# A four-layer graph network in one kernel: scores of two layers moved into the values' buffer, masks taken from the codes

## The chip, the cores and the metric

The kernel runs on one core of a Trainium2 chip, as one program with one launch. The metric is the device time in microseconds (us); lower is better. Four of the core's engines do the arithmetic: TensorE (PE) multiplies matrices and turns tiles, VectorE (DVE) and ScalarE (ACT) work element by element, GpSimd (POOL) does small things here. Each engine takes its instructions in a fixed order and waits for the others by semaphores. SyncE (SP) issues nearly all DMA transfers, also in a fixed order.

## The reference

32 graphs of 512 nodes with 256 features go through four layers. Each layer normalises x, takes the positive part, runs a graph attention over the same adjacency matrix, and adds the result to x. What matters for this change is the attention of layers 1 and 2, whose logits are a sum of one number per row and one per column, and the masks:

```python
    # layer 1
    src = Wh @ a1
    dst = Wh @ a2
    e = src[:, :, None] + dst[:, None, :]
    e = jnp.where(e > 0, e, ALPHA * e)
    e = jnp.where(adj > 0, e, NEG_INF)
    attention = jax.nn.softmax(e, axis=-1)
    h_prime = jnp.einsum('bij,bjf->bif', attention, Wh)

    # layer 2
    logits = s[:, :, None] + d[:, None, :]
    e = jnp.where(adj != 0, jnp.exp(-jax.nn.leaky_relu(logits, negative_slope=ALPHA)), jnp.zeros((), dtype=Hh.dtype))
    rowsum = jnp.sum(e, axis=-1, keepdims=True)
    h_prime = jnp.einsum('bnm,bmo->bno', e, Hh) / rowsum
```

Layers 0 and 3 have full products for their logits; they use the same adjacency. The adjacency holds only 0 and 1.

## The kernel before, in words

**Work and tiles.** A graph has 4 tiles of 128 nodes (NT = 4). All arithmetic is in 32-bit floats; masks and codes are bfloat16. Per graph, PE makes the products of layer 0 (bank_f, bank_v0, bank_q, bank_a0, bank_z, bank_o), the values of layers 1 and 2 (bank_v1, bank_v2) with their attentions (bank_a1, bank_a2), and the products of layer 3 (bank_f3, bank_v3, bank_s3, bank_w3, bank_a3). Results land in eight banks of PSUM, and a bank is free again once ACT or DVE has read it out.

**The order.** The code of a graph doesn't issue instructions; it records operations with an assumed cost, what they come after, and which buffers they use (`op`). A planner (class `Plan`) then lists the operations of all 32 graphs together: each has a due time that is worked back from its graph's end, the most urgent one that is ready goes first, and a buffer must be free when its first user starts. It tries several distances between the graphs' due times and keeps the one that its own replay likes best. Several graphs are thus in flight at once (FLIGHT = 5), and any edit of operations or buffers can change the order of everything else. On the chip each engine keeps the planned order.

**Buffers.** Most tiles of 4 KB a partition share one pool of pages (PAGES = 35): x, e (half of the attention matrix each), masks, hT and so on. The values of a layer lie in one of four buffers v of [128, 4, 259] floats (VALUES = 4): two columns ahead (LEAD = 2), 256 values, and a last column of ones that gives the row sums of the attention matmul. Layers 0 to 2 read it from column 2 on, 257 columns; layer 3 uses all 259.

**Scores of layers 1 and 2.** The weights l1_aug and l2_aug have 258 columns: 256 for the values and two more for the two numbers per node. One matmul group per tile (`scored_values`, L669) gives all 258 columns in a bank. ACT copies 256 of them to v (L676), DVE copies the two last to a score buffer (L673), one of five [128, 132] tiles, one for each graph in flight. From there `leaky_exp_t` makes the row of 512 column numbers on all partitions. For the first two and last two graphs PE turns the scores, tile by tile, into a bank (bank_r, L693). For the others DVE turns blocks of 32x32 (sT, L697), a small DMA collects the row in DRAM (L701), and another spreads it to all partitions (L706). Then ACT makes Prelu of the row plus a bias per partition, which is the other score (L710), and the exponential (L713).

**Codes and masks.** Per graph, DVE turns the adjacency into codes (L511), DMAs transpose them (codeT, L514), and DVE makes mask0 (L522), mask1 (L931) and mask3 (L1001), a page each. Layer 1 keeps or crushes an element of e by a minimum with mask1 (L934); layer 2 multiplies with "code is not zero" straight from codeT (L961).

Of the kernel before, what the change touches and what calls it, by code (L numbers as in the profile page):

```python
# [11 lines left out]
F32 = mybir.dt.float32  # L12
# [3 lines left out]
AF = mybir.ActivationFunctionType  # L16
ALU = mybir.AluOpType
PSUM = bass.MemoryType.PSUM

P = 128  # L20
EPS = 1e-5
ALPHA = 0.2
NEG_INF = -(2.0**53)
TINY = 2.0**-100
HUGE = 2.0**100
LEAST = 2.0**-126
LOWEST = -3.0e38

# [177 lines left out]
def kernel(  # L206
# [31 lines left out]
    nc = tc.nc  # L238
# [2 lines left out]
    HC = H // P  # L241
    HALF = H // 2
    FLIGHT = 5
    PAGES, VALUES = 35, 4
    TURNED = 2
    LEAD = 2

# [88 lines left out]
    def load(dst, src, *keys):  # L336

        loads.append(prepare("G", G_LOAD, [], lambda: nc.gpsimd.dma_start(out=dst() if callable(dst) else dst, in_=src),
                             *keys, size=P * HC * H * 4 if keys else 4096))
        return loads[-1]  # L340

    def rows_of(w):
        return w.rearrange("(c p) k -> p c k", p=P)
# [9 lines left out]
    def transposed(w_sb, dst, after, *keys):  # L353
        done = []
        for c in range(HC):
            key = f"bank{next(banks)}"

            def turn(c, key):
                for r in range(HC):
                    nc.tensor.transpose(W[key][:, r * P : (r + 1) * P], w_sb()[:, r, c * P : (c + 1) * P], ident)  # L360

            def out_of(c, key):
                nc.vector.tensor_copy(dst()[:, c, :], W[key][:, : HC * P])

            a = prepare("PE", pe(nt=HC), after, partial(turn, c, key), key, *keys)
            done.append(prepare("V", V_ADD, [a], partial(out_of, c, key), key, *keys))
        return done

    def product(dst, wT, rhs, cols, after, *keys):

        done = []
        for d in range(HC):
            key = f"bank{next(banks)}"

            def multiply(d, key):
                for c in range(HC):
# [38 lines left out]
    for n, dst, w, key in (("w0", w0_s, w0, "raw9"), ("att", att_s, att_w, "raw10")):  # L415
# [8 lines left out]
    l1_sb, l2_wt, l3_sb, a12_sb, wt3, awt, m3_sb, l3_w1_sb = (raw(f"raw{i}") for i in range(8))  # L424
    l3_wide = raw("raw8", H + 2)
    a = [load(l1_sb, rows_of(l1_w), "raw0")]
    ready["l1"] = transposed(l1_sb, lambda: l1_aug[:, :, :H], a, "raw0")
    a += [load_column(l1_ac, l1_a.rearrange("n o -> (n o)"))]
    ready["l1"] += product(lambda d: l1_aug[:, d, H : H + 2], l1_sb,
                           lambda c: l1_ac.rearrange("p (o c) -> p c o", o=2)[:, c, :], 2, a, "raw0")  # L430
    a = [load(l2_aug[:, :, :H], rows_of(l2_w))]
    a = ready["l2"] = a + transposed(lambda: l2_aug[:, :, :H], l2_wt, a, "raw1")
    a = a + [load_column(l2_ac, l2_a.rearrange("o n -> (o n)"))]
    ready["l2"] = a + product(lambda d: l2_aug[:, d, H : H + 2], l2_wt,
                              lambda c: l2_ac.rearrange("p (o c) -> p c o", o=2)[:, c, :], 2, a, "raw1")

    t = transposed(l3_sb, wt3, [load(l3_sb, rows_of(l3_w), "raw2")], "raw2", "raw4")
# [17 lines left out]
    for i in range(VALUES):  # L455
        v = const.tile([P, NT, LEAD + H + 1], F32, tag=f"v{i}", name=f"v{i}")
        nc.gpsimd.memset(v[:, :, LEAD + H :], 1.0)
        v_bufs.append(v)

    score_bufs = []  # L460
    for i in range(FLIGHT):
        s = const.tile([P, P + NT], F32, tag=f"scores{i}", name=f"scores{i}")
        nc.gpsimd.memset(s, 0.0)
        score_bufs.append(s)


    def graph(b, adj_before, x_before):
# [4 lines left out]
        def op(engine, cost, after, emit, *keys, size=0, weights=()):  # L472
            return plan.op(engine, cost, after, emit, b, T.uses(keys) + W.uses(weights), size)

        def two(g):
            return slice(2 * g, 2 * g + 2)
# [7 lines left out]
        def e(l, c):  # L484

            return T[f"e{l}_{c // 2}"][:, c % 2, :]
# [21 lines left out]
                o["after"] += got_adj[-1:]  # L508

        def classes(g):  # L510
            nc.vector.tensor_scalar(T["code"][:, two(g), :], T["adj"][:, two(g), :], -1.0, 2.0, ALU.max, ALU.min)  # L511

        def turn_code(t):
            nc.sync.dma_start_transpose(out=T["codeT"][:, :, t * P : (t + 1) * P], in_=T["code"][:, t, :])  # L514
# [4 lines left out]
            coded += [op("D", D_TURN, [code], partial(turn_code, t), "code", "codeT") for t in (2 * g, 2 * g + 1)]  # L519

        def mask0():
            nc.vector.tensor_scalar(T["mask0"], T["codeT"], 1.0, TINY, ALU.is_equal, ALU.max)  # L522

        m0 = op("V", V_HALF, coded, mask0, "codeT", "mask0")

# [126 lines left out]
            return (lambda x: [sums[x][0]] if x in sums else list(after),  # L652
                    lambda x: d(sums[x][1]) if x in sums else b(*plain[x]))

        def scores_of():

            return score_bufs[T.places["slot"]["number"]]

        def scored_values(l, hs, w_aug, ready):


            cols = w_aug.shape[2]
            vs, ss = [], []
            for t in range(NT):
                key = f"bank_v{l}{t}"

                def product(t, key):
                    for c in range(HC):
                        nc.tensor.matmul(T[key][:, :cols], T[f"hT{l}"][:, c, t * P : (t + 1) * P],  # L669
                                         w_aug[:, c, :], start=(c == 0), stop=(c == HC - 1))  # L670

                def scores(t, key):
                    nc.vector.tensor_copy(scores_of()[:, 32 * t : P + 1 + t : P - 31 * t], T[key][:, H:cols])  # L673

                def values(t, key):
                    nc.scalar.copy(T[f"v{l}"][:, t, LEAD : LEAD + H], T[key][:, :H])  # L676

                a = op("PE", pe(n258=4), [hs[t]] + ready, partial(product, t, key), key, f"hT{l}")
                ss.append(op("V", V_TINY, [a], partial(scores, t, key), key))
                vs.append(op("A", A_HALF, [a], partial(values, t, key), key, f"v{l}"))  # L680
            return vs, ss

        def leaky_exp_t(l, ss, sign):

            turned = b < TURNED or b >= B - TURNED
            key = f"bank_r{l}" if turned else f"row{l}"
            line = []  # L690

            def turn(t):
                nc.tensor.transpose(T[key][:, t * P : (t + 1) * P],  # L693
                                    scores_of()[:, 32 * t : 32 * t + 1].to_broadcast([P, P]), ident)

            def squares():
                nc.vector.transpose(T[f"sT{l}"], scores_of()[:, :P])  # L697

            def collect():
                line.append(dram.tile([N], F32, tag=f"row_{T.places['slot']['number']}", name=f"row{l}_{b}"))  # L700
                nc.sync.dma_start(out=line[0].rearrange("(t g j) -> g t j", t=NT, j=32),  # L701
                                  in_=T[f"sT{l}"][0:P:32, :].rearrange("g (t j) -> g t j", t=NT))

            def spread():
                d = line[0]
                nc.sync.dma_start(out=T[key][:, 0, :], in_=bass.AP(tensor=d.tensor, offset=d.offset, ap=[[0, P], [1, N]]))  # L706

            def leaky(c):
                row = T[key] if turned else T[key][:, 0, :]
                nc.scalar.activation(e(l, c), row, AF.Prelu, bias=scores_of()[:, P + c : P + c + 1], alpha=ALPHA)  # L710

            def exp(c):
                nc.scalar.activation(e(l, c), e(l, c), AF.Exp, scale=sign)  # L713

            a = None
            if turned:
                for t in range(NT):
                    a = op("PE", pe(nt=1), [ss[t], a], partial(turn, t), key)
            else:
                a = op("V", V_SQUARES, ss, squares, f"sT{l}")  # L720
                a = op("D", D_OUT, [a], collect, f"sT{l}")
                a = op("D", D_SPREAD, [a], spread, key, size=P * N * 4)
            ls = [op("A", A_PRELU if turned else A_PRELU2, [a], partial(leaky, c), key, f"e{l}_{c // 2}") for c in range(NT)]
            return [op("A", A_EXP, [x], partial(exp, c), f"e{l}_{c // 2}") for c, x in enumerate(ls)]

        def attend(l, es, vs, use):
# [200 lines left out]
            xs += [op("V", V_ADD, [a], partial(add_z, 2 * g + j), "z0", "x") for j in range(2)]  # L927


        def mask1():  # L930
            nc.vector.tensor_scalar(T["mask1"], T["codeT"], HUGE, TINY, ALU.mult, ALU.max)  # L931

        def masked1(c):
            nc.vector.tensor_tensor(e(1, c), e(1, c), T["mask1"][:, c, :], ALU.min)  # L934

        hs = normed(1, xs)
        m1 = op("V", V_HALF, [m0, hs[0]], mask1, "codeT", "mask1")
        vs, ss = scored_values(1, hs, l1_aug, ready["l1"])
        es = leaky_exp_t(1, ss, 1.0)
        es = [op("V", V_MASK, [a, m1], partial(masked1, c), "mask1", f"e1_{c // 2}") for c, a in enumerate(es)]  # L940

        def second(t, a, key):
            def sums():
# [10 lines left out]


        hs = normed(2, xs)
        vs, ss = scored_values(2, hs, l2_aug, ready["l2"])
        es = leaky_exp_t(2, ss, -1.0)

        def masked2(c):  # L960
            nc.vector.scalar_tensor_tensor(e(2, c), T["codeT"][:, c, :], 0.0, e(2, c), ALU.not_equal, ALU.mult)  # L961
# [224 lines left out]
```

## Time and profile before

| what | us |
|---|---|
| device time, median of 3 runs | 2376.73 |
| lowest and highest of the 3 | 2376.35, 2377.58 |
| device time of the profiled execution | 2375.45 |
| its span, from first to last instruction | 2373.7 |
| busy POOL | 251.6 |
| longest wait of PE in the page's groups | 6.0 (all of L736's together) |

A profile page gives busy time per engine as a share of the span, the span in slices, the chain of work that ended last, and groups of instructions by line and shape, each with its count, busy time, mean duration in ns and the idle time just before it with what ended it. Timelines list instructions in order of time. A busy PE isn't PE at its peak: matmuls are pipelined, so the distance from the start of one to the start of the next says more than the duration of each (a 257-column matmul of L736 has a mean duration of 381 ns).

### The profile page before, as it was taken

Reading aid. Unit: us, or ns where it says so; the run is one execution under the profiler, and the core shown is the slowest. Engines: PE = TensorE matmul, PEld = TensorE weight load, DVE = VectorE, ACT = ScalarE, POOL = GpSimd, SP = SyncE. Lnnn points to the kernel's source line nnn. Section 1 sums busy time; section 2 is a strip of 40 time slices with the busy share of each in tenths; the row PEclk is TensorE's granted clock in tenths of the full one; section 3 lists DMA queues with packets and bytes.
Section 4 is the critical chain, followed back from the end, with each engine's and each line's share of the span. In section 5 each row is a group of like instructions: output and inputs, shape, how many; then the busy total and the mean of one; then the engine's idle time right before and its main releaser. Section 6 shows DMA issues by size and latency. Waiting matters only on the chain.

```text
span 2373.7 us, 36569 instructions
## 1 busy us (share of the span) xinstructions
PE 2347.7 (99%) x11590; PEld 1985.6 (84%) x11590; DVE 2056.8 (87%) x6330; ACT 1720.1 (72%) x3386; POOL 251.6 (11%) x319
## 2 busy tenths in 40 slices
PE   7999999999999999999999999999999999999998
PEld 5887888888888888888888888888888888888887
DVE  6787899888898888988888988889888889888799
ACT  4566777777777777777777777777777777766785
POOL 3000010111001010101110111001011100100110
PEclk9999999999999999999999999999999999999999
DMA  7421332333333233332323334233233333321221
GB/s 188 94 54 30 87 86 65 85 79 69 85 70 89 69 67 87 78 84 70 85 61 85 74 72 87 65 85 78 66 88 77 71 83 74 89 54 41 49 47 43
DMA packets 432017, 178.72 MB, mean 75 GB/s; under 512 B 386288, under 2 KB 403824, under 8 KB 431824
## 3 DMA queue, kind: packets, MB, share of 16 engines
q1 hardware_dynamic: 426464, 158.03, 29.8%
q0 software_dynamic: 5216, 18.23, 2.3%
q8 instruction: 92, 1.51, 0.3%
q14 instruction: 101, 0.83, 0.1%
q10 hardware_dynamic: 144, 0.13, 0.0%
HBM read 67.64 MB, written 16.89 MB: 36 GB/s over the span
## 4 chain that ended last, share of the span: by engine, by line
PE 94%; DVE 3%; ACT 2%; DMA 0%; issue 0%; SPq 0%; POOL 0%; DVEq 0%; ACTq 0%
PE bank_a L736 35%; PE bank_z L893 9%; PE bank_v L669 9%; PE bank_o L911 5%; PE bank_s3p L1025 5%; PE bank_q0p L848 4%; PE bank_f3p L757 4%; PE bank_v0p L783 4%; PE bank_f0p L757 4%; PE bank_w3p L783 4%; PE bank_q0q L848 3%; PE bank_s3q L1025 3%; PE bank_v3p L783 2%; PE bank_v3q L783 2%; ACT e L710 1%; ACT e L713 0%
## 5 line engine op out<-in xcount | busy, mean ns | idle before, releaser
L736 PE MATMUL bank_a<-v,e 128*128 128x257 f32 (+1 forms) x4096 | 979.8, 381 | 6.0 <-DVE e L823 3.0
L736 PEld LDWEIGHTS bank_a<-v,e 128*128 128x128 f32 x4096 | 758.3, 190 | 155.3 <-issue 55.3
L566 ACT COPY hT<-planesT 128x512 uint16<-128x512 uint16 x508 | 380.8, 766 | 52.0 <-DMA planesT<-planes 51.6
L539 POOL TENSOR_TENSOR rstd<-ve,mhalf 128x2 f32<-128x2 f32 x256 | 215.9, 871 | 1875.1 <-DVE ve L536 1584.4
L546 ACT ACTIVATE xn<-x,off,rstd 128x256 f32<-128x256 f32 x512 | 276.0, 596 | 39.2 <-DVE off L542 39.0
L669 PE MATMUL bank_v<-l_aug,hT 128*128 128x258 f32 x1024 | 252.8, 381 | 2.1 <-ACT e L710 1.1
L893 PE MATMUL bank_z<-e,y 128*128 128x512 f32 x512 | 240.6, 592 | 0.0
L551 DVE COPY planes<-xn 128x512 uint16<-128x512 uint16 x508 | 205.7, 418 | 23.0 <-DMA planesT<-planes 17.2
L669 PEld LDWEIGHTS bank_v<-l_aug,hT 128*128 128x128 f32 x1024 | 191.7, 190 | 30.5 <-ACT e L710 1.5
L532 DVE BATCH_NORM_STATS2 st<-x 128x6 f32<-128x256 f32 x512 | 209.0, 408 | 4.1 <-DMA x<-in_x_dram 4.0
L710 ACT ACTIVATE e<-row,scores 128x512 f32<-128x512 f32 x224 | 150.7, 713 | 16.3 <-DMA row<-row 16.0
L893 PEld LDWEIGHTS bank_z<-e,y 128*128 128x128 f32 x512 | 96.9, 190 | 68.0 <-issue 57.9
L713 ACT ACTIVATE e<-e 128x512 f32<-128x512 f32 x256 | 150.3, 624 | 0.0
L676 ACT COPY v<-bank_v 128x256 f32<-128x256 f32 x256 | 90.2, 376 | 71.5 <-PE bank_v L669 67.7
L911 PE MATMUL bank_o<-w_sb,zT 128*128 128x256 f32 x512 | 116.2, 379 | 0.0
L1032 DVE SCALAR_TENSOR_TENSOR e<-bank_s3p,v,mask 128x256 f32<-128x256 f32 x256 | 111.2, 476 | 2.7 <-PE bank_s3p L1025 1.9
L533 DVE BATCH_NORM_AGGREGATE mv<-st 128x2 f32<-128x6 f32 x512 | 93.1, 182 | 17.5
L911 PEld LDWEIGHTS bank_o<-w_sb,zT 128*128 128x128 f32 x512 | 97.0, 190 | 13.4
L1077 ACT ACTIVATE e<-e 128x512 f32<-128x512 f32 x128 | 78.1, 629 | 22.7 <-DVE e L1074 22.0
L915 DVE SCALAR_TENSOR_TENSOR z<-bank_o,rs,b_sb 128x256 f32<-128x256 f32 x128 | 56.0, 479 | 40.7 <-PE bank_o L911 40.1
L974 ACT ACTIVATE y<-bank_a,rs 128x256 f32<-128x256 f32 x128 | 54.7, 476 | 49.4 <-DVE rs L970 25.9
L1071 ACT ACTIVATE e<-e,zero 128x512 f32<-128x512 f32 x128 | 84.9, 711 | 6.6 <-DVE crest L1049 6.6
(189 smaller groups left out, 4414.9 us busy)
## 6 DMA issues: line engine op xcount, KB each, us to landing
adj<-in_adj_dram SPq DMA_DIRECT2D x128, 256.0 KB
x<-in_x_dram SPq DMA_DIRECT2D x31, 512.0 KB
out_dram<-y POOLq DMA_DIRECT2D x31, 512.0 KB, 3.5
row<-row SPq DMA_DIRECT2D x56, 256.0 KB
planesT<-planes SPq DMA_TRANSPOSE x508
codeT<-code SPq DMA_TRANSPOSE x128
crest<-crest SPq DMA_TRANSPOSE x64
row<-sT SPq DMA_DIRECT2D x56, 2.0 KB
```

The source lines that it names most:

```text
L532: nc.vector.bn_stats(T[f"st{l}"][:, t, :], T["x"][:, t, :])
L539: nc.gpsimd.tensor_tensor(T[f"rstd{l}"][:, two(g)], T[f"ve{l}"][:, two(g)], mhalf[:, two(g)], ALU.pow)
L546: nc.scalar.activation(T[f"xn{l}"][:, t, :], T["x"][:, t, :], AF.Relu, bias=T[f"off{l}"][:, t : t + 1], scale=T[f"rstd{l}"][:, t : t + 1])
L551: nc.vector.tensor_copy(T[f"planes{l}_{t}"], bits)
L566: nc.scalar.copy(bits[:, :, :, t * P : (t + 1) * P], T[f"planesT{l}_{t}"].rearrange("p (b c) n -> p b c n", b=2))
L669: nc.tensor.matmul(T[key][:, :cols], T[f"hT{l}"][:, c, t * P : (t + 1) * P], w_aug[:, c, :], start=(c == 0), stop=(c == HC - 1))
L736: nc.tensor.matmul(T[key][:, : LEAD + H + 1 - lead], e(l, c)[:, t * P : (t + 1) * P], T[f"v{l}"][:, c, lead:], start=(c == 0), stop=(c == ...
L757: nc.tensor.matmul(p[:, : N // 2], w[:, x - 1, :], right(x), start=fresh, stop=True, skip_group_check=True)
L783: nc.tensor.matmul(p[:, j * k : (j + 1) * k], right(x)[:, j * P : (j + 1) * P], w[:, x - 1, :], start=fresh and j == 0, stop=True, skip_gr ...
L893: nc.tensor.matmul(T[f"bank_z{k}"], T["y0"][:, c, k * P : (k + 1) * P], e(0, c), start=(c == 0), stop=(c == NT - 1))
L911: nc.tensor.matmul(T[key][:, j * H : (j + 1) * H], T["zT"][:, k, t * P : (t + 1) * P], w1_sb[:, k, :], start=(k == 0), stop=(k == HC - 1))
L1025: nc.tensor.matmul(p[:, j * N // 2 : (j + 1) * N // 2], left(x)[:, j * P : (j + 1) * P], right(x), start=fresh and j == 0, stop=True, skip ...
```

## The change

Four things are changed together. The two score columns move to the front of the weights, so that they land in the two leading columns of the values' buffer by the same ACT copy that brings the values; the score buffers and DVE's score copies are gone, and what read the scores reads v. The codes are the adjacency times 2^96 instead of a clamped adjacency, so that layer 1 can take its minimum with max(code, 2^-100) in one operation, and mask1 is gone. The pool of pages has one page less, and there are five buffers of values instead of four. The dependences follow: the transposes and Prelus wait for ACT's copies, where they waited for DVE's.

```diff
-HUGE = 2.0**100
+HUGE = 2.0**96
...
-    PAGES, VALUES = 35, 4
+    PAGES, VALUES = 34, 5
...
-    ready["l1"] = transposed(l1_sb, lambda: l1_aug[:, :, :H], a, "raw0")
+    ready["l1"] = transposed(l1_sb, lambda: l1_aug[:, :, 2:], a, "raw0")
...
-    ready["l1"] += product(lambda d: l1_aug[:, d, H : H + 2], l1_sb,
+    ready["l1"] += product(lambda d: l1_aug[:, d, 0:2], l1_sb,
...
-    score_bufs = []
-    for i in range(FLIGHT):
-        s = const.tile([P, P + NT], F32, tag=f"scores{i}", name=f"scores{i}")
-        nc.gpsimd.memset(s, 0.0)
-        score_bufs.append(s)
...
         def classes(g):
-            nc.vector.tensor_scalar(T["code"][:, two(g), :], T["adj"][:, two(g), :], -1.0, 2.0, ALU.max, ALU.min)
+            nc.vector.tensor_scalar(T["code"][:, two(g), :], T["adj"][:, two(g), :], HUGE, None, ALU.mult)
...
         def mask0():
-            nc.vector.tensor_scalar(T["mask0"], T["codeT"], 1.0, TINY, ALU.is_equal, ALU.max)
+            nc.vector.tensor_scalar(T["mask0"], T["codeT"], HUGE, TINY, ALU.is_equal, ALU.max)
...
-                def scores(t, key):
-                    nc.vector.tensor_copy(scores_of()[:, 32 * t : P + 1 + t : P - 31 * t], T[key][:, H:cols])
-
                 def values(t, key):
-                    nc.scalar.copy(T[f"v{l}"][:, t, LEAD : LEAD + H], T[key][:, :H])
+                    nc.scalar.copy(T[f"v{l}"][:, t, :cols], T[key][:, :cols])
 
                 a = op("PE", pe(n258=4), [hs[t]] + ready, partial(product, t, key), key, f"hT{l}")
-                ss.append(op("V", V_TINY, [a], partial(scores, t, key), key))
                 vs.append(op("A", A_HALF, [a], partial(values, t, key), key, f"v{l}"))
-            return vs, ss
+            return vs
...
             def turn(t):
                 nc.tensor.transpose(T[key][:, t * P : (t + 1) * P],
-                                    scores_of()[:, 32 * t : 32 * t + 1].to_broadcast([P, P]), ident)
+                                    T[v][:, t, 0:1].to_broadcast([P, P]), ident)
 
             def squares():
-                nc.vector.transpose(T[f"sT{l}"], scores_of()[:, :P])
+                nc.vector.transpose(T[f"sT{l}"].rearrange("p (t j) -> p t j", t=NT), T[v][:, :, 0:32])
...
             def leaky(c):
                 row = T[key] if turned else T[key][:, 0, :]
-                nc.scalar.activation(e(l, c), row, AF.Prelu, bias=scores_of()[:, P + c : P + c + 1], alpha=ALPHA)
+                nc.scalar.activation(e(l, c), row, AF.Prelu, bias=T[v][:, c, 1:2], alpha=ALPHA)
...
-                    a = op("PE", pe(nt=1), [ss[t], a], partial(turn, t), key)
+                    a = op("PE", pe(nt=1), [vs[t], a], partial(turn, t), key, v)
             else:
-                a = op("V", V_SQUARES, ss, squares, f"sT{l}")
+                a = op("V", V_SQUARES, vs, squares, f"sT{l}", v)
...
-        def mask1():
-            nc.vector.tensor_scalar(T["mask1"], T["codeT"], HUGE, TINY, ALU.mult, ALU.max)
-
         def masked1(c):
-            nc.vector.tensor_tensor(e(1, c), e(1, c), T["mask1"][:, c, :], ALU.min)
+            nc.vector.scalar_tensor_tensor(e(1, c), T["codeT"][:, c, :], TINY, e(1, c), ALU.max, ALU.min)
 
         hs = normed(1, xs)
-        m1 = op("V", V_HALF, [m0, hs[0]], mask1, "codeT", "mask1")
-        vs, ss = scored_values(1, hs, l1_aug, ready["l1"])
-        es = leaky_exp_t(1, ss, 1.0)
-        es = [op("V", V_MASK, [a, m1], partial(masked1, c), "mask1", f"e1_{c // 2}") for c, a in enumerate(es)]
+        vs = scored_values(1, hs, l1_aug, ready["l1"])
+        es = leaky_exp_t(1, vs, 1.0)
+        es = [op("V", V_MASK, [a], partial(masked1, c), "codeT", f"e1_{c // 2}") for c, a in enumerate(es)]
```

The weights of layer 2 are shifted like those of layer 1, and layer 2 calls `scored_values` and `leaky_exp_t` in the same new way.

More of the change, by code (lines that the diff above doesn't have):

```diff
@@ L426 @@
     a = [load(l1_sb, rows_of(l1_w), "raw0")]
-    ready["l1"] = transposed(l1_sb, lambda: l1_aug[:, :, :H], a, "raw0")
+    ready["l1"] = transposed(l1_sb, lambda: l1_aug[:, :, 2:], a, "raw0")
     a += [load_column(l1_ac, l1_a.rearrange("n o -> (n o)"))]
-    ready["l1"] += product(lambda d: l1_aug[:, d, H : H + 2], l1_sb,
+    ready["l1"] += product(lambda d: l1_aug[:, d, 0:2], l1_sb,
                            lambda c: l1_ac.rearrange("p (o c) -> p c o", o=2)[:, c, :], 2, a, "raw0")
-    a = [load(l2_aug[:, :, :H], rows_of(l2_w))]
-    a = ready["l2"] = a + transposed(lambda: l2_aug[:, :, :H], l2_wt, a, "raw1")
+    a = [load(l2_aug[:, :, 2:], rows_of(l2_w))]
+    a = ready["l2"] = a + transposed(lambda: l2_aug[:, :, 2:], l2_wt, a, "raw1")
     a = a + [load_column(l2_ac, l2_a.rearrange("o n -> (o n)"))]
-    ready["l2"] = a + product(lambda d: l2_aug[:, d, H : H + 2], l2_wt,
+    ready["l2"] = a + product(lambda d: l2_aug[:, d, 0:2], l2_wt,
                               lambda c: l2_ac.rearrange("p (o c) -> p c o", o=2)[:, c, :], 2, a, "raw1")
@@ L653, in block_sums @@
                     lambda x: d(sums[x][1]) if x in sums else b(*plain[x]))
-        def scores_of():
-            return score_bufs[T.places["slot"]["number"]]
         def scored_values(l, hs, w_aug, ready):
             cols = w_aug.shape[2]
-            vs, ss = [], []
+            vs = []
             for t in range(NT):
@@ L670, in product, with leaky_exp_t @@
                                          w_aug[:, c, :], start=(c == 0), stop=(c == HC - 1))
-                def scores(t, key):
-                    nc.vector.tensor_copy(scores_of()[:, 32 * t : P + 1 + t : P - 31 * t], T[key][:, H:cols])
                 def values(t, key):
-                    nc.scalar.copy(T[f"v{l}"][:, t, LEAD : LEAD + H], T[key][:, :H])
+                    nc.scalar.copy(T[f"v{l}"][:, t, :cols], T[key][:, :cols])
                 a = op("PE", pe(n258=4), [hs[t]] + ready, partial(product, t, key), key, f"hT{l}")
-                ss.append(op("V", V_TINY, [a], partial(scores, t, key), key))
                 vs.append(op("A", A_HALF, [a], partial(values, t, key), key, f"v{l}"))
-            return vs, ss
-        def leaky_exp_t(l, ss, sign):
+            return vs
+        def leaky_exp_t(l, vs, sign):
             turned = b < TURNED or b >= B - TURNED
             key = f"bank_r{l}" if turned else f"row{l}"
-            line = []
+            line, v = [], f"v{l}"
             def turn(t):
                 nc.tensor.transpose(T[key][:, t * P : (t + 1) * P],
-                                    scores_of()[:, 32 * t : 32 * t + 1].to_broadcast([P, P]), ident)
+                                    T[v][:, t, 0:1].to_broadcast([P, P]), ident)
             def squares():
-                nc.vector.transpose(T[f"sT{l}"], scores_of()[:, :P])
+                nc.vector.transpose(T[f"sT{l}"].rearrange("p (t j) -> p t j", t=NT), T[v][:, :, 0:32])
             def collect():
@@ L717, in leaky_exp_t @@
                 for t in range(NT):
-                    a = op("PE", pe(nt=1), [ss[t], a], partial(turn, t), key)
+                    a = op("PE", pe(nt=1), [vs[t], a], partial(turn, t), key, v)
             else:
-                a = op("V", V_SQUARES, ss, squares, f"sT{l}")
+                a = op("V", V_SQUARES, vs, squares, f"sT{l}", v)
                 a = op("D", D_OUT, [a], collect, f"sT{l}")
                 a = op("D", D_SPREAD, [a], spread, key, size=P * N * 4)
-            ls = [op("A", A_PRELU if turned else A_PRELU2, [a], partial(leaky, c), key, f"e{l}_{c // 2}") for c in range(NT)]
+            ls = [op("A", A_PRELU if turned else A_PRELU2, [a], partial(leaky, c), key, v, f"e{l}_{c // 2}") for c in range(NT)]
             return [op("A", A_EXP, [x], partial(exp, c), f"e{l}_{c // 2}") for c, x in enumerate(ls)]
@@ L956, in graph @@
         hs = normed(2, xs)
-        vs, ss = scored_values(2, hs, l2_aug, ready["l2"])
-        es = leaky_exp_t(2, ss, -1.0)
+        vs = scored_values(2, hs, l2_aug, ready["l2"])
+        es = leaky_exp_t(2, vs, -1.0)
         def masked2(c):
```

## The prediction

> **What bounds the kernel now.** I read the page first, then TensorE's timeline over the whole span, then the stretches in which it has gaps, then the groups by shape. The page's busy shares, and the first pieces of its chain:
>
> ```profile
> span 2373.7 us, 36569 instructions
> PE 2347.7 (99%) x11590; PEld 1985.6 (84%) x11590; DVE 2056.8 (87%) x6330; ACT 1720.1 (72%) x3386; POOL 251.6 (11%) x319
> ...
> PE 94%; DVE 3%; ACT 2%; DMA 0%; issue 0%; SPq 0%; POOL 0%; DVEq 0%; ACTq 0%
> ```
>
> PE carries 94% of the chain. [...] So I priced PE by its pace instead, from the chain in order of time:
>
> ```profile
> 107.11 3.45 PE bank_o L911 x16
> ...
> 334.22 12.22 PE bank_a L736 x56
> ...
> 522.03 2.62 PE bank_v L669 x12
> ...
> 1859.03 12.14 PE bank_a L736 x56
> ```
>
> 12.14 us for 56 is 217 ns for one 257-column matmul, 3.45/16 is 216 ns for 256 columns, and it is the same at 334 us as at 1859 us. The median distance from one start to the next, kind by kind: 217 (257 and 258 columns), 218 (259), 216 (256), 429 (512), 111 (128 and 129). Times the counts: attention 3072 x 217 + 1024 x 218 = 889.8 us; values of layers 1 and 2 1024 x 217 = 222.2; bank_z 512 x 429 = 219.6; bank_o 512 x 216 = 110.6; bank_f 882 x 216 = 190.5; bank_q and bank_s 1764 x 216 = 381.0; the 2660 of 128 or 129 columns x 111 = 295.3; set-up, first graph and bank_r some 33. Sum 2342.1 us. The rest of the span is 2373.7 - 2342.1 = 31.6: 9.1 before the first matmul, 16.7 in gaps or slow matmuls, 5.8 at the end (from the last one's pace to the last instruction). Where the 16.7 lie, by stretches of 75 us: 4.75 in 0 to 75 (net of early matmuls under their kind's median), 3.4 in 150 to 225, 0.5 in 300 to 375, 0.15 around 1760, 0.6 in 2025 to 2100, 7.3 from 2175 on; from 375 to 1725 us every stretch has less than 0.02. The windows agree (columns: stretch, its length, busy us and count of PE, weight load, DVE, ACT, POOL, clock, DMA share, GB/s):
>
> ```profile
> 150.00:225.00 75.00, 72.37 (x365) 60.94 (x364) 58.54 (x181) 47.68 (x95) 5.00 (x7) 1.00 0.15 27
> ...
> 900.00:975.00 75.00, 75.00 (x375) 63.92 (x374) 66.47 (x206) 57.09 (x113) 8.82 (x11) 1.00 0.31 75
> ...
> 2250.00:2325.00 75.00, 72.22 (x391) 63.06 (x390) 68.67 (x220) 58.35 (x126) 7.72 (x9) 1.00 0.21 43
> ```
>
> So in the long middle no other engine costs anything, and a change that leaves PE's instructions alone can only win or lose at the two ends. The largest gap of the ramp, on ACT and then PE:
>
> ```profile
> 192.94 1.35 ACT L710 ACTIVATE e<-row,scores 128x512 f32<-128x512 f32 x2
> 194.16 1.16 ACT L713 ACTIVATE e<-e 128x512 f32<-128x512 f32 x2
> 195.20 1.34 ACT L710 ACTIVATE e<-row,scores 128x512 f32<-128x512 f32 x2
> 196.42 1.15 ACT L713 ACTIVATE e<-e 128x512 f32<-128x512 f32 x2
> 197.46 0.84 ACT L884 ACTIVATE y<-bank_a,rs 128x256 f32<-128x256 f32 x2
> ...
> 197.99 0.70 PE L736 MATMUL bank_a<-v,e 128*128 128x257 f32 x2 [2.16 <-ACT y L884]
> ```
>
> PE waits for graph 3's tanh, which frees a bank; that tanh stands in ACT's order behind 16 Prelus and exponentials of graphs 1 and 2.
>
> **The change, part by part.** The groups concerned:
>
> ```profile
> L961 DVE SCALAR_TENSOR_TENSOR e<-codeT,e 128x512 f32<-128x512 bf16 x128 | 85.8, 680 | 2.5 <-ACT e L713 1.8
> ...
> L934 DVE TENSOR_TENSOR e<-e,mask 128x512 f32<-128x512 f32 x128 | 82.3, 682 | 3.1 <-ACT e L713 3.0
> ...
> L673 DVE COPY scores<-bank_v 128x2 f32<-128x2 f32 x256 | 35.6, 151 | 15.8 <-ACT v L676 7.6 <-PE bank_v L669 6.6
> ...
> L931 DVE TENSOR_SCALAR mask<-codeT 128x2048 bf16<-128x2048 bf16 x32 | 21.7, 677 | 0.0
> ```
>
> - Removed on DVE: 256 score copies, 35.6 us, and 32 mask1, 21.7 us: 57.3 of 2056.8, so DVE falls from 87% to 84%. Beside a full PE in the middle this is worth 0; it is worth something only at the ends.
> - masked1 becomes the form of L961: 680 against 682 ns, 0. [...]
> - The codes lose one of two operations over the same 1024 elements: 683 ns kept as the dear end, 64 x 0.1 us saved as the cheap one, all hidden: 0. The masks of layers 0, 2 and 3 keep their cost.
> - ACT's values copy takes 258 columns for 256. L1012 copies 258 in 375 ns, L676 256 in 376: 0.
> - The two score columns now lead the weights, so PE writes the same 258 columns; transposes onto bank_r stay 32 x 109 ns. The attention still reads 257 columns from column 2. PE's 2342.1 stay.
> - The 32x32 transposes read with a stride of 259 elements instead of a packed tile. No row shows that; nearest is L697's 301 ns. Bounds 0 and +0.3 us each on DVE, taken 0: a second 301 ns on 56 of them is 17 us, less than the 57.3 removed.
> - The new wait: row transposes, bank_r transposes and the Prelu biases need ACT's copy (376 ns, in ACT's order) where they needed a 151 ns copy on DVE. That is 0.2 us more in itself, plus what stands ahead in ACT's order. Behind it on DVE stand masks and sums, behind the row's two DMAs on SP the next transposes of planes and codes. One such route of layer 2 in the old trace: squares at 972.57, its two DMAs at 972.89 and 976.69, the Prelus at 980.30, the first matmul on them at 984. By the instruction order and the paces above, the work PE has between the last bank_v of a layer and its first attention matmul is 20.0 to 23.5 us before and 19.2 to 21.8 after (graphs 10, 11, 20, 21). The route costs 0.4 copy + 0.3 + 3.8 + 3.6 + two Prelus and two exponentials 2.4 + mask 0.7 = 11.2. Some 8 us stay for queueing, so 0.
> - One page less, one v buffer more: in the changed order graph 2's layer 1 uses the fifth buffer while four are held. POOL drops five memsets of 0.2 us and gains one, at 1 to 2 us, when it waits until 7.47 anyway: 0.
>
> What does count is the new order that the planner draws from all this. Up to the first attention matmul the engines' orders are unchanged, so the 9.1 and the 3.1 us wait for the first mask stay. That wait also drops the clock: most of the next ten matmuls run some 210 ns slow. [...] These 4.75 are kept but for 0.6 of the small waits at 60 to 66 us. In the ramp, graph 3's tanh now stands ahead of graph 2's Prelus and behind joins and value copies. To size this I counted, in each order, ACT's work (at the durations of the rows) from the PE result that it needs up to an instruction, against PE's work before the user of that instruction: the worst user in the ramp is 4.4 us short before, and has 0.1 us to spare after. Of 3.4 us I take away 3.0, and leave 0.4 for an addition in graph 3's bank_f that is 0.3 us short. The 0.5 at 308 us is a bank_f that waits for DVE's addition, the 0.6 at 2077 an attention that waits for layer 2's mask on DVE; there the same count for DVE goes from 0.9 short to 0.3 spare. I let both go (bounds: 0 and 1.1 us).
>
> The tail: 7.3 us of gaps with DVE 92% busy. Some 16 score copies and one mask1 leave it, 3 us of DVE at most; but the last copies end at 2274, and the chain after 2285 is Prelus, sums and stores that stay. Against it, both last graphs take the transpose route four times, and at 2272 to 2274 ACT's copy came 1.6 us after DVE's. Steps with under 1.5 us of PE work between producer and user fall from 132 to 120 in the last 150 us. The count above has the worst user of ACT 6.3 us short before and 6.2 after, of DVE 2.0 and 1.9. Bounds: 3 us gained, 4 x 1.6 = 6.4 lost; I take 1 gained.
>
> Sum: 0.6 + 3.0 + 0.5 + 0.6 + 1.0 = 5.7 us. The profiled execution took 2375.45 (1.75 around its span), so it would take 2369.8; from the median of 2376.73, 1.3 above that one, 2371.0.
>
> **Rivals.**
> - B, the stalls only move: another tight place appears wherever one goes, PE is full anyhow. For it: 99% busy; against: the tanh is plainly reordered. 2376.7, within 2.
> - C, the tail shortens too, because DVE is its bound and each removed copy waits for PE: 3 us in the tail instead of 1, and the small start waits wholly gone: 2368. Against: the removed work isn't in the last 90 us.
> - D, slower: the score route is late. Deciding point: values copy to attention over some 19 us instead of 11.2, by ACT's queue (57 of 75 us busy) and SP's. ACT already waited 21 of 56 times for the row, 16.0 us in all, without any cost to PE. If each of 56 routes cost PE 0.3 us, 17 us less the 5.7: 2388.
> - [...]
>
> **Numbers.** My forecast A 0.50 (2368.5 to 2373.5), C 0.20, B 0.18, D 0.12. Measurements of this kernel tell 0.2%, that is 4.75 us, from no change: under 2372.0 is faster, over 2381.5 slower. Two thirds of A (0.33) and C (0.20) are faster: 0.53; a third of A and B: 0.35; D: 0.12. The range reaches over C and B and leaves out D: 2366 to 2379.
>
> **What would show it.** PE's paces unchanged and the middle without gaps; no 2.2 us gap on PE at some 195 us with a tanh behind Prelus; the 3.1 us gap at 28.5 still there; DVE busy some 1999 us; the tail's gaps 5 to 8 us. Wrong would be: any repeated gap in the middle before an attention matmul whose Prelu waited for the row (D), or a tail over 10 us.

## The result, and the profile after

| | before | after |
|---|---|---|
| device time, median (us) | 2376.73 | 2370.59 |
| lowest and highest of 7 runs each | 2375.1, 2377.88 | 2366.34, 2372.2 |
| device time of the profiled execution | 2375.45 | 2372.2 |
| its span | 2373.7 | 2370.4 |

The ratio of the times is 0.9973, with a 95% interval of 0.9962 to 0.9983: 6.1 us faster. The profiled execution of after is the slowest of its seven, so the two spans differ by 3.3 us only; the runs of after scatter by 5.9 us, those of before by 2.8.

The page of after, its span, busy shares and the engines of its chain:

```profile
span 2370.4 us, 36184 instructions
PE 2347.1 (99%) x11590; PEld 1985.5 (84%) x11590; DVE 2029.9 (86%) x6042; ACT 1724.8 (73%) x3386; POOL 253.1 (11%) x315
...
PE 94%; DVE 3%; DMA 1%; ACT 1%; issue 0%; POOL 0%; SPq 0%; DVEq 0%; ACTq 0%; POOLq 0%
```

PE has the same 11590 matmuls and the same 94% of the chain; 288 instructions are gone from DVE. The paces, in the chain of after in order of time (start, length, piece):

```profile
108.18 3.45 PE bank_o L896 x16
...
333.94 12.14 PE bank_a L721 x56
```

The same 216 and 217 ns a matmul as before. The windows of after (columns as before: PE, weight load, DVE, ACT, POOL, clock, DMA share, GB/s):

```profile
150.00:225.00 75.00, 74.76 (x365) 63.01 (x364) 61.66 (x190) 54.76 (x109) 7.12 (x9) 1.00 0.18 34
900.00:975.00 75.00, 75.00 (x377) 63.95 (x376) 66.14 (x193) 57.18 (x114) 8.04 (x9) 1.00 0.34 78
2250.00:2325.00 75.00, 72.82 (x393) 63.23 (x392) 68.09 (x213) 59.72 (x126) 7.55 (x9) 1.00 0.20 42
```

PE's busy time in the ramp rose from 72.37 to 74.76 us of 75, in the tail's window from 72.22 to 72.82; in the middle it was full and is full. To put a figure on every stretch I took, for both traces, the distance from each matmul's start to the next less the usual distance of its kind. With one set of rounded distances for both (2340.2 us in sum) before has 18.6 us of such excess; its 16.7 in the prediction came from medians.

| excess on PE (us) | before | after | moved | predicted |
|---|---|---|---|---|
| up to the first matmul | 9.1 | 9.3 | +0.2 | 0 |
| 0 to 75 | 4.8 | 5.5 | +0.7 | -0.6 |
| 75 to 225, the ramp | 3.5 | 0.8 | -2.6 | -3.0 |
| 225 to 375 | 0.6 | 0.3 | -0.4 | -0.5 |
| 375 to 2025 | 1.5 | 2.7 | +1.3 | 0 |
| 2025 to 2175 | 0.8 | 0.6 | -0.2 | -0.6 |
| 2175 to the last matmul, the tail | 7.5 | 5.2 | -2.3 | -1.0 |
| after the last matmul | 5.8 | 5.8 | 0 | 0 |

The ramp, in the timeline of after (start, length, engine, line):

```profile
187.37 0.91 ACT L869 ACTIVATE y<-bank_a,rs 128x256 f32<-128x256 f32 x2 [0.17 <-DVE rs L866]
...
189.28 1.32 ACT L695 ACTIVATE e<-row,v 128x512 f32<-128x512 f32 x2
...
193.70 5.36 PE L721 MATMUL bank_a<-v,e 128*128 128x257 f32 x24
```

Graph 3's tanh (L869) now runs at 187.37, ahead of the Prelus, where it ran at 197.46 behind them; PE goes through 24 attention matmuls where it stood still for 2.2 us.

### The profile page after: what moved, and what is told of

It reads as the page before. It is cut to its first block, busy times and chain, and to the rows that moved or that the text cites. A ratio compares the mean times of both kernels' runs of the same rounds, so it can differ in the third digit from the quotient of the medians.

```text
span 2370.4 us, 36184 instructions
## 1 busy us (share of the span) xinstructions
PE 2347.1 (99%) x11590; PEld 1985.5 (84%) x11590; DVE 2029.9 (86%) x6042; ACT 1724.8 (73%) x3386; POOL 253.1 (11%) x315
## 4 chain that ended last, share of the span: by engine, by line
PE 94%; DVE 3%; DMA 1%; ACT 1%; issue 0%; POOL 0%; SPq 0%; DVEq 0%; ACTq 0%; POOLq 0%
PE bank_a L721 36%; PE bank_z L878 9%; PE bank_v L658 9%; PE bank_o L896 5%; PE bank_s3p L1006 4%; PE bank_q0p L833 4%; PE bank_f3p L742 4%; PE bank_v0p L768 4%; PE bank_w3p L768 4%; PE bank_f0p L742 4%; PE bank_s3q L1006 3%; PE bank_q0q L833 3%; PE bank_v3p L768 2%; PE bank_v3q L768 2%; DMA planesT<-planes 1%; DVE st L526 0%
## 5 line engine op out<-in xcount | busy, mean ns | idle before, releaser
L721 PEld LDWEIGHTS bank_a<-v,e 128*128 128x128 f32 x4096 | 769.4, 190 | 164.6 <-issue 53.9
L695 ACT ACTIVATE e<-row,v 128x512 f32<-128x512 f32 x224 | 153.0, 715 | 4.5 <-DMA row<-row 4.3
L698 ACT ACTIVATE e<-e 128x512 f32<-128x512 f32 x256 | 156.2, 629 | 0.0
L662 ACT COPY v<-bank_v 128x258 f32<-128x258 f32 x256 | 95.9, 375 | 81.5 <-PE bank_v L658 79.8
L869 ACT ACTIVATE y<-bank_a,rs 128x256 f32<-128x256 f32 x128 | 56.8, 470 | 83.0 <-DVE rs L866 83.0
L841 ACT ACTIVATE e<-e 128x512 f32<-128x512 f32 x93 | 58.5, 629 | 56.8 <-DVE e L850 56.8
L1058 ACT ACTIVATE e<-e 128x512 f32<-128x512 f32 x128 | 76.8, 634 | 18.5 <-DVE e L1055 18.5
```

The lines of the kernel that those rows point to most:

```text
L721: nc.tensor.matmul(T[key][:, : LEAD + H + 1 - lead], e(l, c)[:, t * P : (t + 1) * P], T[f"v{l}"][:, c, lead:], start=(c == 0), stop=(c == ...
```

## The experiments

The change holds three things: two kinds of work taken off DVE (score copies, mask1) and a fifth buffer of values. Each also makes the planner draw another order for all engines. So the question was whether the time came from the work that left DVE (R in the expectations), or from the buffers and the order drawn with them (O); later whether moving the scores (S) or the distance between the graphs (T) decides the tail. The planner chose 40 us between the graphs' due times for before, 38 for after. All of these kernels compute the whole reference. The two columns in the middle are the excess on PE in 150 to 225 us and from 2175 us on, taken as above from the profiled execution:

| kernel | distance | ramp | tail | median, beside before's (us) | ratio, 95% interval |
|---|---|---|---|---|---|
| before | 40 | 3.5 | 7.5 | 2376.73 | |
| after | 38 | 0.6 | 5.2 | 2370.59, 2376.73 | 0.9973, 0.9962 to 0.9983 |
| mask1_silent | 40 | 5.2 | 8.6 | 2377.14, 2376.17 | 1.0001, 0.9992 to 1.0009 |
| dve_put_back | 38 | 0.6 | 6.0 | 2370.2, 2376.17 | 0.9975, 0.9965 to 0.9985 |
| buffers_only | 38 | 0.8 | 9.0 | 2376.3, 2376.17 | 1.0003, 0.9995 to 1.0011 |
| after_old_pools | 42 | 8.1 | 8.0 | 2376.99, 2376.17 | 1.0008, 1.0 to 1.0016 |
| scores_and_buffers | 40 | 0.3 | 6.2 | 2369.54, 2376.11 | 0.9972, 0.9962 to 0.9982 |
| masks_and_buffers | 38 | 0.3 | 4.1 | 2368.83, 2376.11 | 0.9969, 0.9958 to 0.9981 |
| before_apart38 | 38 | 4.4 | 10.7 | 2385.29, 2376.11 | 1.0033, 1.0021 to 1.0046 |
| buffers_apart40 | 40 | 0.6 | 7.8 | 2372.7, 2376.11 | 0.9990, 0.9982 to 0.9998 |
| after_apart40 | 40 | 0.5 | 7.1 | 2371.15, 2375.49 | 0.9984, 0.9977 to 0.9990 |
| after_early_adj | 40 | 1.5 | 7.3 | 2369.98, 2375.49 | 0.9978, 0.9971 to 0.9986 |
| masks_early_adj | 38 | 0.1 | 9.2 | 2371.2, 2375.49 | 0.9984, 0.9977 to 0.9992 |
| buffers_mask1_silent | 38 | 0.8 | 9.0 | 2377.45, 2375.19 | 1.0006, 0.9997 to 1.0014 |

### Work off DVE, with the order held fixed

mask1_silent is before with the codes times 2^96 and layer 1 masked from them. The planner's operation for mask1 stays, but issues nothing, so that every engine keeps the order of before:

```diff
         def mask1():
-            nc.vector.tensor_scalar(T["mask1"], T["codeT"], HUGE, TINY, ALU.mult, ALU.max)
+            pass
...
-            nc.vector.tensor_tensor(e(1, c), e(1, c), T["mask1"][:, c, :], ALU.min)
+            nc.vector.scalar_tensor_tensor(e(1, c), T["codeT"][:, c, :], TINY, e(1, c), ALU.max, ALU.min)
```

> The kernel before in its own order, but mask1 is planned and not issued: layer 1 masks from the codes times 2^96 as in the change. It takes 21.7 us off DVE and moves no instruction. Theory O: 2376.5, within 1, the gap at some 195 us stays. Rival R: 22 of 57 parts of 6 us, so 2374.4.

No gain: 1.0001, and the gaps of before are all there, the one of the ramp among them. PE's timeline of mask1_silent:

```profile
192.81 1.90 PE L736 MATMUL bank_a<-v,e 128*128 128x257 f32 x8
196.87 4.05 PE L736 MATMUL bank_a<-v,e 128*128 128x257 f32 x11 [2.16 <-ACT y L884]
```

The wait for graph 3's tanh is the same 2.16 us as in before. Eleven matmuls then take 4.05 us, where before needed 1.35 for five: seven of them come 427 to 431 ns apart. The granted clock is 0.50 there, as the windows of the last section show. In 2250 to 2325 us it averages 0.98, where before has 1.00: PE's waits from 2175 us on have the lengths of before's, and the tail is 8.6 us for 7.5.

dve_put_back is the mirror of it: after, in after's own order, with 512 small copies put back on DVE, one behind each of the normalisation's statistics:

```diff
+                nc.vector.tensor_copy(spare[:, 0:2], mhalf[:, 0:2])
```

> The changed kernel in its own order, with a small DVE copy (2 columns, some 0.07 us each beside its neighbours, 512 of them, some 35 to 70 us busy) issued after every node statistic: about the DVE work that the change took off is put back, no other instruction moves. Theory O: 2371, within 1.5. Rival R: 2376, within 1.5.

Its page:

```profile
PE 2346.6 (99%) x11590; PEld 1987.6 (84%) x11590; DVE 2056.7 (87%) x6554; ACT 1721.3 (73%) x3386; POOL 267.6 (11%) x315
```

DVE is busy as long as before the change (2056.8), and the gain is whole: 0.9975 against after's 0.9973. So the relief of DVE as such is not what made the kernel faster; R falls on both sides. Neither run covers all of it: mask1_silent takes off 22 of the 57 us, and the copies put back wait for nothing from PE, as the score copies did. At 87% beside a PE that is full, relief of DVE bought nothing: 22 us of instructions fewer on DVE were worth nothing that shows in 2377.14 beside 2376.17.

### The fifth buffer alone, and everything but it

```diff
-    PAGES, VALUES = 35, 4
+    PAGES, VALUES = 34, 5
```

> The kernel before with five buffers of values and 34 pages, nothing else. Theory O (the gain is the new order that the fifth buffer lets the planner draw): 2371 us, within 2, the 2.2 us gap of TensorE at some 195 us gone, DVE still busy some 2057 us. Rival R (the gain is the 57 us of work taken off DVE): 2376.5, within 1. Rival P (any new order has its own stalls, the sign is chance): anything from 2370 to 2382.

> The changed kernel with the old pools, 35 pages and four buffers of values; DVE's work is off as in the change. Theory O: 2375 to 2377, a gap over 1.5 us in the ramp (150 to 225 us). Rival R: 2371, within 1. Rival P: anything from 2370 to 2382.

after_old_pools is after with this line turned back. The line has two numbers, and no run changes one alone. But the planner is part of the kernel: given 40 us and four buffers, the planner of before draws the same order with 34 pages as with 35, and likewise with five buffers, so the page that was given up changes nothing by itself there. Without the fifth buffer the whole of the rest is worth nothing (2376.99), and PE waits in the ramp again. The waits of PE in after_old_pools, 150 to 225 us (waiting line, what for: us in all, times, longest):

```profile
PE bank_q0p L833 <- ACT e L847: 2.5, 1, 2.5
PE bank_f0p L742 <- ACT fa L750: 0.9, 2, 0.5
```

With the buffer alone the ramp is clean (0.8 us for 3.5), as O had it. But the time is 2376.3, where O had 2371 within 2: the 2.7 us won in the ramp are spent elsewhere in this order, as P allows. Its tail costs 1.5 us more than before's, the middle 1.1, the first 75 us 0.8, and 2025 to 2175 us 0.5. The largest place, in the timeline of ACT and then of PE in buffers_only:

```profile
2268.28 0.78 ACT L566 COPY hT<-planesT 128x512 uint16<-128x512 uint16 x1
...
2269.42 0.77 ACT L566 COPY hT<-planesT 128x512 uint16<-128x512 uint16 x1
2270.04 1.22 ACT L974 ACTIVATE y<-bank_a,rs 128x256 f32<-128x256 f32 x3
2271.11 1.60 ACT L977 ACTIVATE r<-bank_a,rs 128x256 f32<-128x256 f32 x4
```

```profile
2271.68 1.14 PE L669 MATMUL bank_v<-l_aug,hT 128*128 128x258 f32 x4 [2.71 <-ACT r L977]
```

PE wants a bank for its next values. It comes free with a relu (L977) that stands behind two copies of hT (L566) and three activations (L974) in ACT's order: the same kind of wait as the one that left the ramp.

### Each kind of work with the fifth buffer

scores_and_buffers is after with codes, mask0 and mask1 as before; masks_and_buffers is before with the new codes, no mask1, and five buffers, and the planner plans anew for each.

> The kernel before with the scores in the values' buffer and the new pools; codes and mask1 stay as before. Theory O2 (the fifth buffer clears the ramp, and the tail depends on the whole new order): no gap over 1 us from 150 to 225 us, tail (2175 us to the last matmul) anywhere from 5 to 9 us, time 2370 to 2376. Rival S (moving the scores is what shortens the tail): tail under 5.5 us, 2370 to 2371.5.

> The kernel before with layer 1 masked from the codes, no mask1, and the new pools; the scores stay in their own buffers. O2: no gap over 1 us from 150 to 225 us, tail anywhere from 5 to 9 us, 2370 to 2376. Rival S: tail as with five buffers alone, 8 to 9 us, 2375.5 to 2377.

Both are as fast as after within the intervals, with half of its edits. O2 had 2370 us at the least for both, and for the second a tail of 5 us or more: both went below. So after does not need both kinds of work gone; but the buffer with neither, at the distance that its planner chose, gave nothing. S had the moved scores as the cause of the shorter tail; the kernel that leaves them where they were has the shortest of all, 4.1 us, and the one that moves them 6.2. S falls.

### The distance between the graphs

The planner's list of distances cut to one:

```diff
-    APART, APART_LAST = [1000.0 * k for k in range(32, 64, 2)], [1000.0 * k for k in (2, 8)]
+    APART, APART_LAST = [40000.0], [8000.0]
```

(38000.0 in before_apart38; buffers_apart40 has the two numbers of the pools as well.)

> The kernel before, its pools and work, but the planner is given 38 us between the due times of the graphs, as it chose itself for the change, where it had chosen 40. Theory O2 (four buffers are what jams the ramp): the ramp keeps gaps of 2 us or more, 2375 to 2380. Rival T (the distance clears the ramp): ramp gaps under 1 us in all, 2372 to 2375.

> The kernel before with five buffers and 34 pages, and 40 us between due times, as the kernel before has it. Theory O2: ramp gaps under 1 us in all, whatever the tail; 2371 to 2377. Rival T: the ramp keeps gaps of 2 us or more, 2376 to 2380.

> The changed kernel with 40 us between the graphs' due times instead of the 38 that its planner chose. Theory O2 (the ramp is cleared by the fifth buffer, the tail is what the order happens to give): under 1 us of gaps from 150 to 225 us; tail anywhere from 4 to 9 us, time 2367 to 2375. Rival T (38 us is part of the gain): ramp gaps of 2 us or more, 2373 to 2378.

38 us alone is no cause of a gain: with four buffers it makes the slowest kernel of all, 2385.29, over O2's range too. And the ramp goes by the buffer at both distances: 4.4 us in before_apart38 against 0.8 in buffers_only at 38, 3.5 against 0.6 at 40. So T falls for the ramp. Whether 38 us adds something to the other edits is not clear: after has 0.9973 and after_apart40 0.9984, with intervals that overlap. buffers_apart40 is the cleanest look at the buffer, since the distance and DVE's work are those of before. Its windows:

```profile
150.00:225.00 75.00, 74.73 (x376) 63.32 (x375) 60.94 (x191) 52.31 (x105) 5.97 (x8) 1.00 0.20 36
...
2250.00:2325.00 75.00, 72.22 (x394) 63.10 (x393) 68.95 (x218) 59.45 (x127) 7.33 (x8) 1.00 0.21 41
```

PE in the ramp goes from 72.37 to 74.73 us, and the tail's window has before's 72.22 to the last digit; its waits there are those of before:

```profile
PE bank_v L669 <- ACT e L710: 1.1, 1, 1.1
PE bank_v L669 <- ACT w L1093: 1.0, 1, 1.0
PE bank_r L693 <- DVE scores L673: 0.8, 1, 0.8
```

The ratio is 0.9990 (0.9982 to 0.9998): 3.4 us by the medians of its row; by the profiles, the ramp gave 2.9. This order loses as well, in places of its own: 2.3 us more excess than before in 375 to 2025 us, 1.5 of it at 1470 us, while 0 to 75 us has 1.3 less. At the same distance the other edits together (after_apart40 against this one) add what lies between 0.9990 and 0.9984, and the intervals overlap.

### The work of one, in the order of the other

buffers_only and masks_and_buffers both have 38 us and five buffers, and their medians lie 7.5 us apart. buffers_mask1_silent takes buffers_only with its order fixed and gives it the other's instructions (the edits of mask1_silent on top of the two numbers of the pools).

> The instruction order of the kernel with five buffers alone (2376.3 us, with a wait of 2.7 us of bank_v at 2268.7 for ACT's copy behind a relu, and a tail of 9.0 us of gaps), held fixed, with the work of the other variant: codes times 2^96, no mask1, layer 1 masked from codeT. With the planner's own order for that work the time was 2368.8 and the tail 4.1 us. If the order decides: 2375 to 2378, the same 2.7 us wait and a tail of 8 to 9.5 us. If the work that left DVE decides at this place: 2369 to 2371, and the tail falls to 4 to 5 us. In between, 2372 to 2374, both share in it. The whole reference is computed.

The waits of PE from 2175 us on, in buffers_mask1_silent:

```profile
PE bank_v L669 <- ACT r L977: 2.7, 1, 2.7
PE bank_a L736 <- ACT e L1077: 1.6, 3, 0.8
```

and in masks_and_buffers:

```profile
PE bank_r L693 <- DVE scores L673: 0.5, 1, 0.5
PE bank_f3p L757 <- DVE fa L772: 0.4, 1, 0.4
```

The same instructions on every engine, 32 empty operations in the plan apart, and 2377.45 against 2368.83 us. The tail is 9.0 us as in buffers_only (the five largest gaps up to 2301 us agree to 0.01 us each), not 4.1. So between these two the order decides, not mask1's work. (Of the 8.9 us between the two profiled spans the tail has 4.9; 2.8 lie in the first 75 us, which differ by up to 2.7 us between two kernels of one order.)

### The first mask

What is left at the start is one wait, nearly as long in both kernels. PE's timeline of after, and then of after_early_adj:

```profile
31.80 2.48 PE L721 MATMUL bank_a<-v,e 128*128 128x257 f32 x5 [3.22 <-DVE e L808]
```

```profile
28.01 1.13 PE L724 MATMUL bank_a<-v,e 128*128 128x257 f32 x4 [0.33 <-DVE e L811]
```

Graph 0's first attention waits for a mask, behind it codes that are transposed by DMAs issued at 20.10 us, when the adjacency has come. In after_early_adj the x of graphs 2 and 3 is fetched behind graph 0's adjacency, and those DMAs go out at 17.33 us:

```diff
-        got_x = [op("D", D_X, [x_before], partial(fetch_x, ts), "x", "ahead", size=P * H * 4 * (ts.stop - ts.start))
+        got_x = [op("D", D_X, [x_before] + (first_adj if b in (2, 3) else []), partial(fetch_x, ts), "x", "ahead", size=P * H * 4 * (ts.stop - ts.start))
...
+            first_adj.extend(got_adj[1:])
```

> A version that goes for what both kernels leave: the x of graphs 2 and 3 is loaded after the first adjacency, so that the first codes can be turned earlier and the first mask isn't late. Theory O2: the wait for the first mask at some 28 us (3 us, with half clock after it) falls under 1 us; 2364 to 2368 unless the new order puts back more in the tail. Rival E (the turning DMAs set the wait, whenever they are issued): gap at 28 us still over 2 us, 2369 to 2372.

> The same early adjacency on the kernel with new masks and pools and with the scores in their own buffers. Theory O2: 2362 to 2367, tail 3.5 to 6 us. Rival E: 2367 to 2370.

The wait falls to 0.3 us, so E falls here, and 28 to 57 us then has 0.05 us of excess, against 5.1 in after and 4.5 in after_apart40, whose distance this kernel has. Yet its 2369.98 us are over O2's 2368; it gains 1.2 us on after_apart40 by the medians, with overlapping intervals, and none on after. The planner had moved other things as well: 1.5 us of excess in the ramp for 0.5. For masks_early_adj the same edit leaves the wait for the first mask at 1.3 us, as masks_and_buffers has it without the edit, and makes the tail 9.2 us for 4.1 and the time 2371.2 for 2368.83, outside both forecasts. No kernel beats the changed one beyond the intervals.

## Why the prediction was right

2371.0 us were predicted and 2370.59 measured; by the profiled executions it was 5.7 us less, and 3.3 came. Step by step:

- **PE bounds it, and only the ends can move.** Right. The paces are the same. The middle didn't stay quite empty: two gaps, 0.8 us at 1041 and 0.2 at 1623, make 1.0 of its +1.3.
- **The ramp, 3.0 us.** Right in mechanism, place and size: 2.6 in after, 2.9 in buffers_apart40. The prediction put it down to the order, with the fifth buffer as a user; the runs show that the buffer is what the order needs. The six orders drawn with five buffers (the two with the early adjacency aside) have at most 0.8 us there, the three drawn with four buffers 3.5 to 8.1. So P's chance is not what clears the ramp.
- **Work off DVE worth nothing.** Right, as far as the two runs reach. The size of the relief was off: DVE was to fall to 1999 us and fell to 2029.9. The prediction took the rows' busy times from the page's total. Summed instruction by instruction DVE lost 60.6 us, but its records overlap their neighbours, and the total counts each moment once: without the 288 records that left, before's own trace comes to 2028.9 us, only 27.9 less.
- **Same cost of the new forms.** Right. The groups of after:

```profile
L916 DVE SCALAR_TENSOR_TENSOR e<-codeT,e 128x512 f32<-128x512 bf16 x128 | 85.7, 681 | 2.0 <-ACT e L698 1.9
...
L505 DVE TENSOR_SCALAR code<-adj 128x1024 bf16<-128x1024 int32 x64 | 43.6, 681 | 0.0
```

  681 ns for 682 of the old layer 1 mask, and 681 for the codes' 683 with one operation fewer. The strided 32x32 transposes (L682) took 306 ns for 301; ACT's copy of 258 columns (L662) 375.
- **The new wait on ACT's copy costs nothing.** Right, and rival D is out. The group of Prelus that read the row:

```profile
L695 ACT ACTIVATE e<-row,v 128x512 f32<-128x512 f32 x224 | 153.0, 715 | 4.5 <-DMA row<-row 4.3
```

  ACT waited 4.3 us for rows in the whole span, against 16.0 before. PE never waits for one in the middle.
- **The start: kept but for 0.6.** The long wait was kept (3.2 us), but in this profile the term has the wrong sign, +0.7. One of the small waits at 60 to 66 us stayed, and a new one came. PE's waits of after up to 75 us:

```profile
PE bank_a L721 <- DVE e L808: 3.2, 1, 3.2
PE bank_q0p L833 <- ACT e L847: 0.9, 1, 0.9
```

  The 0.9 is at 68.8 us, a bank freed by ACT: the count of ACT's work against PE's cover that sized the ramp was made for the ramp, and not here. How much of this is the order is open: in dve_put_back, which keeps after's order on PE and ACT, the first wait is 1.6 us, the 0.9 is gone, and the stretch has 2.7 us less excess.
- **The small ones at 308 and 2077 us, 0.5 and 0.6.** The first went (0.4); in the place of the second stands 0.34 at 2059, so 0.2.
- **The tail, 1.0 of a gain between 3 and -6.4.** The sign was right, the size too small: 2.3. The worked reason, that a little DVE work leaves it, is not what did it. Before's waits of bank_v for ACT (1.1 and 1.0) and of bank_r for the score copies (0.8) are gone; in their place, the waits of after:

```profile
PE bank_a L721 <- DVE e L942: 1.0, 1, 1.0
PE bank_f3p L742 <- ACT v L993: 0.8, 1, 0.8
PE bank_a L721 <- DVE e L916: 0.5, 1, 0.5
```

  Over the kernels run here this term is anything from 4.1 to 10.7 us, set by the order that was drawn. Rival B, that stalls only move, is what buffers_only did; rival C, that DVE's relief shortens the tail, had its size nearly right, but its reason is at most a part: without mask1 neither fixed order has a shorter tail, and masks_and_buffers, which keeps every score copy, has the shortest; only dve_put_back, with 6.0 us for after's 5.2, leaves room for it.

That the sum held to 0.4 us owes something to chance. Start and middle went 2.6 us the wrong way, and the tail made up 1.3 of that. And the median of after lies 1.6 us below its profiled execution, where the prediction carried over the 1.3 us above that before has: 2.9 us, about what the profiled execution fell short. The runs scatter with TensorE's clock: of before's 45 runs beside after_apart40, 27 had a mean granted clock of 0.999 and took 2374.5 us on average, 12 had 0.998 and took 2376.3, 6 had 0.997 and took 2376.8; the seven of after had 0.999 or 1.000. One spell more of 3.41 us at half clock went with 1.7 us more in mask1_silent's ramp (5.2 us of excess for 3.5); by my estimate it lowers a run's mean clock by 0.0007 (half of 3.41 in 2374 us). So the gap of the ramp could cost more in some runs of before than in its profile, where no spell followed it; how much of the 6.1 us that is was not measured. The first mask's wait differs too, 1.4 us in masks_and_buffers' profile, 3.4 in after's.

Two things stay open beside that. Which operation's place turns the tail was not found: the edits change costs and dependences at once, and the planner's list moves as a whole. And after's order with four buffers was not tried, as that order puts work where only a fifth buffer is free.

## What to carry to other kernels

Where one engine is full and a planner draws the order, measure an edit's work and an edit's order apart: keep the order and drop the instruction, then keep the instructions and change the order. The gap that came from too few buffers was gone, or down to 0.6 us, in every order here that had one more; what is won or lost at the tail belongs to one drawing of the order, and can eat the first gain whole. Don't subtract the busy time of removed small instructions from an engine's total: the records overlap, and here less than half of it came off (26.9 us, where 60.6 us of instructions had gone).

## What the runs showed of the hardware

The half clock after a wait did not go by the wait's length alone here. In after, the 3.2 us wait for the first mask is followed by six matmuls 427 to 431 ns apart, and the granted clock is 0.50 from 31.62 to 35.03 us; in before, a wait of 3.0 us for it is followed by 0.50 from 32.21 to 35.63 us. But the wait in the ramp, 2.16 us in mask1_silent as in before, cost nothing further in before, and 1.7 us more in mask1_silent.

The clock in the traces shows where the two differ. Here are two stretches of mask1_silent, then three of before (columns as in the windows above; the clock is the third number from the end):

```profile
194.55:197.97 3.42, 1.26 (x6) 0.98 (x6) 2.04 (x6) 3.42 (x8) 0.00 (x0) 1.00 0.00 0
197.97:201.38 3.41, 3.41 (x10) 2.68 (x9) 3.36 (x7) 2.88 (x6) 0.00 (x0) 0.50 0.00 0
```

```profile
192.63:196.05 3.42, 3.20 (x17) 2.53 (x15) 2.79 (x7) 3.42 (x7) 0.00 (x0) 1.00 0.00 0
196.05:199.46 3.41, 1.47 (x7) 1.30 (x8) 2.03 (x6) 3.41 (x8) 0.00 (x0) 1.00 0.00 0
199.46:202.87 3.41, 3.41 (x18) 2.97 (x17) 3.31 (x8) 3.01 (x7) 0.00 (x0) 1.00 0.00 0
```

In mask1_silent the clock is 1.00 in the stretch with the wait and 0.50 in the next 3.41 us, though PE went on 1.1 us before that. In before it is 1.00 in all three, with the 2.16 us wait across the first two. So the same wait cost nothing in one profile and 1.7 us in the other; what decides between the two was not shown.
